# A two-layer graph network: contiguous query tiles, operands of layer 1 written in their final form by layer 0, and unit sums divided in the output stage

## The chip, the cores and the metric

The kernel runs on one core of one Trainium2 chip. A core has a matrix engine (TensorE, PE in the profile; its weight loads are PEld), VectorE (DVE), ScalarE (ACT), GpSimd (POOL), and SyncE (SP), which here only issues DMAs. The metric is device time in microseconds (us), the median over several executions. The kernel before takes 15601.34 us (three executions, 15598.64 to 15608.1).

## The reference

Two layers act on `x` (3327 nodes × 128 features) with one 0/1 matrix `adj` (3327 × 3327).

```python
# layer 0: attention by cosine over the neighbours
cos = beta[0] * (x @ x.T) / (norm2 @ norm2.T + 1e-07)
x = layernorm(x + softmax(cos + (1.0 - adj) * -1e9, axis=1) @ x)
# layer 1: d = 128, n = 3327, h = 8; q, k, v are reshaped, not transposed
q, k, v = [(x @ W.T).reshape(d, n, h) for W in (Wq, Wk, Wv)]
a = jnp.einsum('dnh,dmh->dnm', q, k) * d ** -0.5 + adj + adj
out = jnp.einsum('dnm,dmh->dnh', softmax(a, axis=2), v).reshape(n, h * d)
x = layernorm(x + out @ Wo.T)
```

Layer 1 is thus 128 dense attentions over 3327 keys, each with vectors of only 8 numbers. Its reshape mixes nodes: row-major, `x @ W.T` (3327 × 1024) is read as 128 × 3327 × 8, so one slice d takes its 3327 × 8 numbers from 26 rows of the product. The output is read back in the same way.

## The kernel before

**Names.** P = 128, N = 3327 nodes, T = 26 tiles, NP = P·T = 3328, so there is one padding node. H = 8, D = 128. Node number p·T + t stands in partition p of tile t, for queries and for keys (`node_rows`, L87, a row every T rows). `every(a, t)` (L125) picks each T-th column. Because tile 25 has only 127 real nodes, loads of it are cut in 112 + 15 partitions (`FULL`, L41) and one more.

**Layer 0** (L166 to L475, 0 to 714 us) makes 26 query tiles in a software pipeline over t: TensorE scores against all keys (`scores`), VectorE scales and masks them and finds the row's minimum, ScalarE takes logarithms and exponentials, TensorE turns the weights and multiplies by x (`turn_weights`, `weigh0`), then residual and layernorm. Each tile loads its rows of adj twice: as float32 (`raw`, SP's queue, `load` L190) and as bfloat16 (`bits`, POOL's queue, `load_bits` L201). `adj_chunk` (L209) turns the bits and stores them as `aT_s`. `project` (L348) multiplies the finished rows by Wq, Wk, Wv in six steps of 512 columns and writes rows of 1024 floats to `q_s`, `k_s`, `v_s`. POOL has almost nothing to do in this stage.

**Preparation** (`prepare`, L811 on, 714 to 989 us). For each of q and k and eight groups of 16 slices d, it loads `nat`, re-orders it on POOL (`by_t`, L819), turns it on TensorE, and splits each number in a high part rounded for TensorE and a low remainder (`high`, `low`), written to `kp_s` and `qp_s` (slice, feature, part, node). Between these steps stand the 33 first steps of the search for maxima (`first_max`).

**Main loop** (L894, 989 to 15505 us). A unit is a query block of three tiles (QB = 384 queries; the last block has two tiles) and a group of four slices d. There are 9 blocks × 32 groups = 288 units, blocks outermost. A unit makes 26 steps j, one key tile each. A step is: scores of four slices (`scores`, L704; the row-wise shift from `shifts`, adj from `add_adj`, L687), exponentials (L917 and L946 on ScalarE; for two slices adj enters as a factor on POOL, L918), and products with the values (`weigh`, L717, two steps later), which gather 9 rows a slice in `acc`: 8 features and, from a column of ones in `vt`, the sum of the weights. The search for row maxima of a later unit runs 33 steps ahead (`search`, TensorE L604, VectorE L619 to L644). It works on pairs of units, and from a known point in the first unit of a pair it needs the second one's keys.

All engines but SP follow the order in which the program is written (`manual_schedule`). SP's DMA issues stand in one queue. They are:

- `load_unit(i + 2)` at j = 2: `kx` (two DMAs), `qx` (four), `vn`; `values` at j = 14 copies `vn` into the nine-wide `vt` on POOL (L565, L566).
- at the end of a unit `take` (L726) copies `acc` to `ot` on ScalarE; at j = 8 of the next unit `values_turn` (L730) turns it by 12 small matmuls; `leave` copies the result, and `finish` (L749, j = 9) takes reciprocals, multiplies on POOL and writes `o_s` in rows of 1024.
- in the last unit of a block, `load_adj_tile` brings one tile of the next block's adj per step, and ScalarE takes its exponential five steps later (`exp_adj_tile`, L519, into `eT`).

**Output stage** (L976 to L1014). Per tile: load 128 rows of `o_s`, eight transposes (L1002), two copies (L147 on VectorE, L145 on ScalarE), eight matmuls with Wo (L1006), residual, layernorm.

Of the kernel before, what the change touches and what calls it, by code (L numbers as in the profile page):

```python
# [21 lines left out]
T = 26  # L22
# [4 lines left out]
HG = P // H  # L27
NG = D // HG
# [12 lines left out]
FULL = ((0, 112), (112, P - 1))  # L41


# [3 lines left out]
def gnn_two_layers(  # L47
# [24 lines left out]
    real = const.tile([P, 1], F32, name="real")  # L72
    nc.vector.tensor_scalar(real, ident[:, P - 1 : P], -1.0, 1.0, op0=ALU.mult, op1=ALU.add)

    q_s = dram.tile([NP, C], F32, name="q_s")
    k_s = dram.tile([NP, C], F32, name="k_s")
    v_s = dram.tile([NP, C], F32, name="v_s")
    o_s = dram.tile([NP, C], F32, name="o_s")

    qp_s = dram.tile([D, H, 2, NP], F32, name="qp_s")  # L80
    kp_s = dram.tile([D, H, 2, NP], F32, name="kp_s")
# [5 lines left out]
    def node_rows(a: bass.AP, t: int, width: int, parts: int = P, first: int = 0):  # L87

        return bass.AP(
            tensor=a.tensor,  # L90
            offset=a.offset + (first * T + t) * width,
            ap=[[T * width, parts], [1, width]],
        )

    def node_parts():

        return [(slice(a, b), T * D) for a, b in FULL] + [(slice(P - 1, P), (T - 1) * D)]

    def node_blocks(a: bass.AP, part: slice, width: int):

        return bass.AP(
            tensor=a.tensor,
            offset=a.offset + part.start * T * D,
            ap=[[T * D, part.stop - part.start], [1, width]],
        )

    def heads(a: bass.AP):

        return bass.AP(
            tensor=a.tensor,  # L110
            offset=a.offset,
            ap=[[HG * N * H, NG], [T * H, P], [N * H, HG], [1, T * H]],
        )

    def load_adj(raw, engine, t: int):

        nc.gpsimd.memset(raw[:, N:NP], PAD)
        if t < T - 1:
            engine.dma_start(raw[:, :N], node_rows(adj, t, N))
        else:  # L120
            for a, b in FULL:
                engine.dma_start(raw[a:b, :N], node_rows(adj, t, N, b - a, a))
            engine.dma_start(raw[P - 1 : P, :N], node_rows(adj, t - 1, N, 1, P - 1))
# [42 lines left out]
    with ExitStack() as l0:  # L166
# [23 lines left out]
        def load(t: int):  # L190
            u = tiles[t]
            u.raw = adj_raw.tile([P, NP], F32, name="raw")
            load_adj(u.raw, nc.sync, t)
            u.xr = ptp.tile([P, D], F32, name="xr", bufs=5)
            if t < T - 1:
                nc.sync.dma_start(u.xr, node_rows(x, t, D))
            else:
                nc.gpsimd.memset(u.xr, 0.0)
                nc.sync.dma_start(u.xr[: P - 1], node_rows(x, t, D, P - 1))

        def load_bits(t: int):  # L201

            u = tiles[t]
            u.bits = adj_raw.tile([P, NP], BF16, name="bits", bufs=2)
            load_adj(u.bits, nc.gpsimd, t)
# [49 lines left out]
        def scores(t: int, j: int):  # L255
# [4 lines left out]
            sc = score_piece(every(xT, t), xT, j)  # L260
# [87 lines left out]
        def project(t: int, k: int):  # L348
# [3 lines left out]
            if i == 0:  # L352
                u.row = ptp.tile([P, C], F32, name="row")
            cols = slice(i * 512, (i + 1) * 512)
            pq = ps_x.tile([P, 512], F32, name="pq")
            nc.tensor.matmul(pq, u.x1T, ws[n][:, cols], start=True, stop=True)
            nc.scalar.activation(
                u.row[:, cols], pq, AF.Copy, scale=float(D) ** -0.5 if n == 0 else 1.0
            )
            if i == 1:  # L360
                nc.sync.dma_start(node_rows((q_s, k_s, v_s)[n], t, C), u.row)

        with tc.manual_schedule(
# [13 lines left out]
            nc.gpsimd.memset(xs[:, T - 1, :], 0.0)  # L377
            xf = xs.rearrange("p t d -> p (t d)")
            for part, width in node_parts():
                nc.sync.dma_start(xf[part, :width], node_blocks(x, part, width))  # L380
# [10 lines left out]
            for t in range(2):  # L391
                load_bits(t)
            ws = []
            for name, wT in (("wq", wqT), ("wk", wkT), ("wv", wvT)):
                wt = big.tile([P, C], F32, name=name)
                nc.sync.dma_start(wt, wT)
                ws.append(wt)


            nc.gpsimd.tensor_mul(xs, xs, xs)  # L400
# [21 lines left out]
            nc.scalar.preload_act_table_set("natural_log_exp_and_others")  # L422

            for t in range(-2, T + 3):
# [4 lines left out]
                for k in range(8):  # L429
                    if k == 0:  # L430
# [13 lines left out]
                        if there(t - 2):  # L444
                            norm_root(t - 2)
                        continue
# [27 lines left out]
                if there(t + 4) and t + 4 > 1:  # L474
                    load_bits(t + 4)  # L475
# [8 lines left out]
    with ExitStack() as at:  # L484
# [17 lines left out]
        vts = [fix.tile([P, 4, T, H + 1], F32, name=f"vt{i}") for i in range(3)]  # L502
        for vt in vts:
            nc.gpsimd.memset(vt[:, :, :, H], 1.0)
            nc.gpsimd.tensor_copy(vt[:, :, T - 1, H], real.to_broadcast([P, 4]))
# [17 lines left out]

        def load_unit(i):
# [8 lines left out]
            kx, qx = u.kx.bitcast(F32), u.qx.bitcast(F32)  # L533
            for c in range(2):
                nc.sync.dma_start(
                    kx.rearrange("(y c) n -> c y n", c=2)[c],
                    kp_s[4 * g : 4 * g + 4].rearrange("d f r n -> (d f r) n"),
                )
                for r in range(2):
                    nc.sync.dma_start(  # L540
                        qx.rearrange("(y r c) n -> r c y n", r=2, c=2)[r, c, :, : u.nq],
# [4 lines left out]
            u.vn = keys.tile([P, 4, T, H], F32, name="vn", bufs=2)  # L546
            nc.sync.dma_start(
                u.vn.rearrange("p g t h -> p g (t h)"),
                bass.AP(
                    tensor=v_s.tensor,  # L550
                    offset=v_s.offset + 4 * g * N * H,
                    ap=[[T * H, P], [N * H, 4], [1, T * H]],
                ),
            )
            u.vt = vts[i % 3]
            if g % 2 == 0:
# [6 lines left out]
        def values(u):  # L563

            nc.gpsimd.tensor_copy(u.vt[:, :, : T - 1, :H], u.vn[:, :, : T - 1])  # L565
            nc.gpsimd.tensor_scalar(  # L566
                u.vt[:, :, T - 1, :H], u.vn[:, :, T - 1], real, None, op0=ALU.mult
# [34 lines left out]
        def max_product(u, dst, a, q, c):  # L602
# [4 lines left out]
                u.kx[rows(a), k0:k1],  # L607
# [118 lines left out]
        def take(u):  # L726
            u.ot = sm.tile([P, QB], F32, name="ot")
            nc.scalar.copy(u.ot[:, : u.nq], acc[:, : u.nq])

        def values_turn(u, dst, start):  # L730

            for q in range(u.nt):
                for c in range(4):
                    k = q * P + 32 * c
                    nc.tensor.matmul(  # L735
                        dst[32 * c : 32 * c + 32, 36 * q : 36 * q + 36],
                        u.ot[:, k : k + 32],
                        nine.rearrange("p h r -> p (h r)"),
                        start=start,
                        stop=True,  # L740
                        tile_position=(0, 32 * c),
                        skip_group_check=True,
                    )

        def leave(u, src):
            u.of = sm.tile([P, QT, 4, H + 1], F32, name="of")
            nc.scalar.copy(u.of[:, : u.nt].rearrange("p q h r -> p (q h r)"), src[:, : 36 * u.nt])

# [304 lines left out]
```

## Time and profile before

| what | us |
|---|---|
| median of three executions | 15601.34 |
| span of the profiled execution | 15611.6 |
| layer 0, last projection ends | 713.63 |
| main loop, first pb | 989.4 |
| output stage, from | about 15510 |

The profiled execution is one of its own, and its span is what the sums of a profile add up to; it is 10.3 us above the median. The page also lists the costliest groups of instructions: line, engine, operation, tile written and tiles read, shapes and count; then busy time in all and mean of one in ns; then the idle time just before them and what ended it.

```profile
L918 POOL TENSOR_TENSOR pb<-pb,eT 128x768 f32<-128x768 f32 (+1 forms) x7488 | 13190.2, 1780 | 656.3 <-ACT pb L917 374.1
L619 DVE TENSOR_REDUCE mx<-m 128x2 f32<-128x1024 f32 x6784 | 8312.5, 1225 | 970.0 <-PE eb L706 568.7
L946 ACT ACTIVATE pa<-ea 128x384 f32<-128x384 f32 (+1 forms) x14976 | 6338.4, 478 | 54.0 <-PE ea L687 14.5
```

The first line reads: 7488 multiplications on POOL, one a step, 1780 ns each, before which POOL was idle for 656 us in all, mostly until ScalarE had made `pb`.

The DMA part of the page gives each kind of transfer, with its size and its time from issue to landing:

```profile
kx<-kp_s SPq DMA_DIRECT2D x576, 832.0 KB, 6.4
vn<-v_s SPq DMA_DIRECT2D x288, 416.0 KB, 3.4
qx<-qp_s SPq DMA_DIRECT2D x1024, 48.0 KB, 4.7
```

### The profile page before, as it was taken

What the parts mean: (1) busy time and instruction counts of PE and PEld (TensorE: products, weight loads), DVE (VectorE), ACT (ScalarE), POOL (GpSimd) and SP (SyncE); (2) the same over time, 40 slices, a digit from 0 to 9 for tenths busy, and PEclk for the clock granted to TensorE, in tenths of its full rate; (3) what the DMA queues carried; (4) which work ended last, traced back from release to release, by engine and by line L of the source; (5) the groups of instructions that cost most, each with busy time, mean ns of one, the idle gap of its engine ahead of it and who ended that gap; (6) DMA issues with size and microseconds to landing.
All of it is one profiled execution on the core that took longest, in us unless ns stands there. A gap on an engine that the chain in (4) does not pass through costs nothing.

```text
span 15611.6 us, 508271 instructions
## 1 busy us (share of the span) xinstructions
PE 15342.4 (98%) x217532; PEld 6892.6 (44%) x217532; DVE 13898.5 (89%) x16311; ACT 12601.3 (81%) x24955; POOL 13899.2 (89%) x9625
## 2 busy tenths in 40 slices
PE   8879999999999999999999999999999999999999
PEld 6634444444444444444444444444444444444555
DVE  7679999999999999999999999999999999998776
ACT  7658888888888888888888888888888888888776
POOL 0059999999999999999999999999999999999886
PEclk9879999999999999999999999999999999999999
DMA  7651111111111111111111111111111111111112
GB/s 207 204 199 47 48 51 53 50 46 50 52 51 46 50 49 54 50 46 50 53 50 46 50 53 49 50 46 56 46 50 46 50 53 50 48 48 60 60 58 75
DMA packets 631082, 973.65 MB, mean 62 GB/s; under 512 B 283568, under 2 KB 545838, under 8 KB 588368
## 3 DMA queue, kind: packets, MB, share of 16 engines
q1 hardware_dynamic: 625024, 918.99, 18.3%
q0 software_dynamic: 3792, 22.15, 0.8%
q8 instruction: 1703, 27.90, 0.8%
q14 instruction: 563, 4.61, 0.1%
HBM read 828.48 MB, written 134.61 MB: 62 GB/s over the span
## 4 chain that ended last, share of the span: by engine, by line
PE 93%; DVE 0%; issue 0%; ACT 0%; DMA 0%; POOL 0%; SPq 0%; POOLq 0%; ACTq 0%; DVEq 0%
PE acc L717 30%; PE ea L687 21%; PE m L604 16%; PE eb L700 13%; PE ea L700 10%; PE ea L706 2%; PE ea L673 1%; PE ea L735 1%; PE eb L706 1%; PE pp L1006 0%; DVE oT L147 0%; DMA qp_s<-low 0%; ACT pa L946 0%; PE tp L157 0%; DVE hid L1008 0%
## 5 line engine op out<-in xcount | busy, mean ns | idle before, releaser
L918 POOL TENSOR_TENSOR pb<-pb,eT 128x768 f32<-128x768 f32 (+1 forms) x7488 | 13190.2, 1780 | 656.3 <-ACT pb L917 374.1
L619 DVE TENSOR_REDUCE mx<-m 128x2 f32<-128x1024 f32 x6784 | 8312.5, 1225 | 970.0 <-PE eb L706 568.7
L917 ACT ACTIVATE pb<-eb 128x768 f32<-128x768 f32 (+1 forms) x7488 | 5894.9, 787 | 2497.9 <-PE eb L706 1784.2
L604 PE MATMUL m<-kx,qx 32*128 32x512 f32 (+1 forms) x23296 | 6873.5, 472 | 80.5 <-DVE mx L619 71.5
L946 ACT ACTIVATE pa<-ea 128x384 f32<-128x384 f32 (+1 forms) x14976 | 6338.4, 478 | 54.0 <-PE ea L687 14.5
L717 PE MATMUL acc<-pb,vt 128*9 128x384 f32 (+1 forms) x29952 | 5901.1, 474 | 0.1
L717 PE MATMUL acc<-pa,vt 128*9 128x384 f32 (+1 forms) x29952 | 5901.1, 474 | 0.0
L640 DVE TENSOR_REDUCE mx<-m 128x1 f32<-128x512 f32 x6400 | 4360.3, 681 | 258.5 <-PE m L604 239.9
L700 PEld LDWEIGHTS <-one 3*128 3x128 bf16 x29952 | 1469.1, 91 | 5634.9 <-issue 4656.0
L687 PE MATMUL ea<-aT,two 128*32 128x384 bf16 (+1 forms) x59904 | 3714.8, 325 | 0.0
L706 PE MATMUL eb<-qx,kx 32*128 32x384 f32 (+1 forms) x14976 | 3422.3, 453 | 0.0
L706 PE MATMUL ea<-qx,kx 32*128 32x384 f32 (+1 forms) x14976 | 3326.9, 434 | 0.0
L604 PEld LDWEIGHTS m<-kx,qx 32*128 32x128 f32 x23296 | 2825.0, 182 | 315.0 <-DVE mx L619 80.0
L700 PE MATMUL ea<-cx,one 3*128 3x384 bf16 (+1 forms) x14976 | 2744.1, 324 | 1.0
L700 PE MATMUL eb<-cx,one 3*128 3x384 bf16 (+1 forms) x14976 | 2464.3, 326 | 4.6 <-ACT pb L917 3.8
L717 PEld LDWEIGHTS acc<-pa,vt 128*9 128x9 f32 x29952 | 1412.0, 91 | 398.9
L717 PEld LDWEIGHTS acc<-pb,vt 128*9 128x9 f32 x29952 | 1411.5, 91 | 386.8 <-POOL pb L918 0.6
L687 PEld LDWEIGHTS <-two 128*32 128x32 bf16 x59904 | 945.2, 95 | 1364.4 <-issue 1171.4
L706 PEld LDWEIGHTS eb<-qx,kx 32*128 32x128 f32 x14976 | 1432.7, 188 | 0.0
L706 PEld LDWEIGHTS ea<-qx,kx 32*128 32x128 f32 x14976 | 1396.3, 182 | 7.3 <-issue 3.7
L644 DVE TENSOR_REDUCE mx<-m 128x2 f32<-128x512 f32 x1088 | 742.9, 683 | 20.6 <-PE m L604 19.3
L630 DVE TENSOR_REDUCE mx<-m 128x4 f32<-128x1024 f32 x288 | 352.8, 1225 | 46.7 <-PE m L604 28.6
(130 smaller groups left out, 4899.0 us busy)
## 6 DMA issues: line engine op xcount, KB each, us to landing
kx<-kp_s SPq DMA_DIRECT2D x576, 832.0 KB, 6.4
vn<-v_s SPq DMA_DIRECT2D x288, 416.0 KB, 3.4
qx<-qp_s SPq DMA_DIRECT2D x1024, 48.0 KB, 4.7
raw<-in_adj_dram SPq DMA_DIRECT2D x25, 1663.5 KB, 6.5
aT_s<-aT SPq DMA_DIRECT2D x26, 832.0 KB, 9.8
bits<-in_adj_dram POOLq DMA_DIRECT2D x25, 831.8 KB, 7.2
aT<-aT_s SPq DMA_DIRECT2D x208, 96.0 KB, 2.1
q_s<-row SPq DMA_DIRECT2D x26, 512.0 KB, 7.6
```

What stands on the lines that cost most here:

```text
L604: nc.tensor.matmul(dst, u.qx[rows(a), q * P : (q + 1) * P], u.kx[rows(a), k0:k1], start=True, stop=True,)
L619: nc.vector.tensor_reduce(u.mx[:, h, qs[0], c], m, axis=AX.X, op=ALU.max)
L630: nc.vector.tensor_reduce(dst, m.rearrange("p a (x k) -> p a x k", x=2), axis=AX.X, op=ALU.max)
L640: nc.vector.tensor_reduce(u.mx[:, a, qs[0], c : c + 1], m, axis=AX.X, op=ALU.max)
L644: nc.vector.tensor_reduce(u.mx[:, a, qs[0] : qs[1] + 1, c], m.rearrange("p (q k) -> p q k", q=2), axis=AX.X, op=ALU.max,)
L687: nc.tensor.matmul(e[r, : u.nq], two[:, r], aT[:, j, : u.nq], start=False, stop=True, tile_position=(0, 32 * c), skip_group_check=True,)
L700: nc.tensor.matmul(e[:, : u.nq], one[r], u.cx[r, : u.nq], start=True, stop=False, skip_group_check=True)
L706: nc.tensor.matmul(e[:, : u.nq], u.kx[rows(a), j * P : (j + 1) * P], u.qx[rows(a), : u.nq], start=False, stop=stop, skip_group_check=True,)
L717: nc.tensor.matmul(acc[32 * h : 32 * h + H + 1, : u.nq], u.vt[:, h, j], pts[h][:, : u.nq], start=(j == 0), stop=(j == T - 1), tile_positio ...
L917: nc.scalar.activation(pt_b[:, :, : u.nq], e_b[:, :, : u.nq], AF.Exp)
L918: nc.gpsimd.tensor_tensor(pt_b[:, :, : u.nq], pt_b[:, :, : u.nq], eT[:, j, : u.nq].unsqueeze(1).to_broadcast([P, 2, u.nq]), ALU.mult,)
L946: nc.scalar.activation(pt_a[:, h, : u.nq], e[:, : u.nq], AF.Exp)
```

## The change

Query tiles become plain: tile t holds nodes 128·t to 128·t + 127, the last 127 (`LAST`) and a copy of the last one. Keys stay in steps of T in the main loop (partition p of tile t is node p·T + t).

Layer 0's `project` splits q and k itself (POOL copies and subtracts) and writes `qn_s`, `kn_s` (part, feature, flat position); Wq and Wk are re-ordered once so that a feature's columns lie together. v is written nine wide with its ones. The bits of adj are cast from `raw` on POOL instead of loaded. The preparation goes. Instead, `gather` copies each group's q and k between tensors in DRAM; a unit of the first block loads its keys in natural order (`kn`, tile `km`), searches on those, and ScalarE orders them into `kx` (`order_keys`, one tile a step, in the unit before), which `keep_keys` writes to `kp_s` for the later blocks. `vt` is loaded by two DMAs of 127 partitions and 1. The unit's nine rows a slice go to `o_s` undivided, by four DMAs, and the output stage takes the reciprocals and multiplies.

```diff
+LAST = N - (T - 1) * P
...
-            for a, b in FULL:
-                engine.dma_start(raw[a:b, :N], node_rows(adj, t, N, b - a, a))
-            engine.dma_start(raw[P - 1 : P, :N], node_rows(adj, t - 1, N, 1, P - 1))
+            engine.dma_start(raw[:LAST, :N], rows_of(adj, t, N, LAST))
+            engine.dma_start(raw[LAST:P, :N], rows_of(adj, t, N, P - LAST, LAST - 1))
...
-            u.bits = adj_raw.tile([P, NP], BF16, name="bits", bufs=2)
-            load_adj(u.bits, nc.gpsimd, t)
+            u.bits = adj_raw.tile([P, NP], BF16, name="bits", bufs=1)
+            nc.gpsimd.tensor_copy(u.bits, u.raw)
...
+            high = ptp.tile([P, 512], F32R, name="high")
+            low = ptp.tile([P, 512], F32R, name="low")
+            nc.gpsimd.tensor_copy(high, row)
+            nc.gpsimd.tensor_tensor(low, row, high.bitcast(F32), ALU.subtract)
+            dst = (qn_s, kn_s)[n]
+            for c, part in enumerate((high, low)):
+                nc.sync.dma_start(
+                    bass.AP(
+                        tensor=dst.tensor,
+                        offset=dst.offset + (c * H + 4 * i) * S2 + t * P * P,
+                        ap=[[P, P], [S2, 4], [1, P]],
+                    ),
+                    part.bitcast(F32).rearrange("p (f s) -> p f s", f=4),
+                )
...
-            nc.gpsimd.tensor_mul(xs, xs, xs)
+            nc.gpsimd.tensor_mul(xs, xn, xn)
...
+        def gather(g):
+
+            def heads_of(a, c, first, n):
+
+                return bass.AP(
+                    tensor=a.tensor,
+                    offset=a.offset + c * H * S2 + 4 * g * N + first,
+                    ap=[[N, 4], [S2, H], [1, n]],
+                )
+
+            for c in range(2):
+                nc.sync.dma_start(qp_s[4 * g : 4 * g + 4, :, c], heads_of(qn_s, c, 0, NP))
+                dst = kq_s[4 * g : 4 * g + 4, :, c]
+                nc.sync.dma_start(dst[:, :, :N], heads_of(kn_s, c, 0, N))
+                nc.sync.dma_start(dst[:, :, N:NP], heads_of(kn_s, c, N - 1, NP - N))
...
             u.vt = vts[i % 3]
+            for first, n, rows in ((0, P - 1, T), (P - 1, 1, N - (P - 1) * T)):
+                nc.sync.dma_start(
+                    u.vt.rearrange("p g t r -> p g (t r)")[first : first + n, :, : rows * R9],
+                    bass.AP(
+                        tensor=v_s.tensor,
+                        offset=v_s.offset + (4 * g * N + first * T) * R9,
+                        ap=[[T * R9, n], [N * R9, 4], [1, rows * R9]],
+                    ),
+                )
...
+        def order_keys(u, j):
+
+            nc.scalar.copy(u.kx[:, j * P : (j + 1) * P], every(u.km.bitcast(F32), j))
+
+        def keep_keys(u):
+
+            nc.sync.dma_start(
+                kp_s[4 * u.g : 4 * u.g + 4].rearrange("d f r n -> (d f r) n"),
+                u.kx.bitcast(F32).rearrange("(y c) n -> c y n", c=2)[0],
+            )
...
-            u.ot = sm.tile([P, QB], F32, name="ot")
-            nc.scalar.copy(u.ot[:, : u.nq], acc[:, : u.nq])
...
+            ot = sm.tile([P, QB], F32, name="ot")
+            nc.scalar.copy(ot[:, : u.nq], acc[:, : u.nq])
+            n = min(u.nq, N - u.b * QB)
+            for h in range(4):
+                nc.sync.dma_start(
+                    bass.AP(
+                        tensor=o_s.tensor,
+                        offset=o_s.offset + (4 * u.g + h) * N + u.b * QB,
+                        ap=[[S2, R9], [1, n]],
+                    ),
+                    ot[32 * h : 32 * h + R9, :n],
+                )
...
+                    if j == 12 and i + 4 < G4:
+                        gather(i + 4)
...
-                    if j == 8 and done is not None:
-                        values_turn(done, free, False)
-                        copies.append(lambda: leave(done, free))
-                    if j == 9 and done is not None:
-                        copies.append(lambda: finish(done))
...
+                    if x is not None and not x.b:
+                        order_keys(x, j)
+                        if j == T - 1:
+                            keep_keys(x)
...
+            rec = work.tile([P, P], F32, name="rec")
+            nc.vector.reciprocal(rec, row[:, H, :])
+            nc.gpsimd.tensor_tensor(
+                row[:, :H, :], row[:, :H, :], rec.unsqueeze(1).to_broadcast([P, H, P]), ALU.mult
+            )
```

Before the loop, the changed kernel gathers groups 0 to 3, loads units 0 and 1, orders the keys of unit 0 on POOL in one copy, and makes the 33 first search steps with the exponentials of block 0's adj between them. In the output stage a tile of `o_s` is loaded as 128 partitions × 9 × 128, in packets of 512 B.

## The prediction

> **What bounds the kernel now.** I read the busy shares, the chain of waits, then the busy time by stretch, one stretch per stage.
>
> ```profile
> PE 15342.4 (98%) x217532; PEld 6892.6 (44%) x217532; DVE 13898.5 (89%) x16311; ACT 12601.3 (81%) x24955; POOL 13899.2 (89%) x9625
> ...
> PE 93%; DVE 0%; issue 0%; ACT 0%; DMA 0%; POOL 0%; SPq 0%; POOLq 0%; ACTq 0%; DVEq 0%
> ```
>
> And the windows: length, busy PE, PEld, DVE, ACT, POOL (with instructions), granted clock, DMA share, GB/s.
>
> ```profile
> 500.00:600.00 100.00, 95.18 (x572) 74.83 (x573) 90.10 (x133) 86.44 (x113) 4.07 (x15) 1.00 0.78 220
> 800.00:850.00 50.00, 21.41 (x86) 15.66 (x86) 27.24 (x42) 13.71 (x27) 8.87 (x3) 0.57 1.00 337
> 1500.00:2500.00 1000.00, 999.88 (x14391) 422.78 (x14388) 921.57 (x1044) 822.88 (x1608) 958.46 (x637) 1.00 0.15 49
> 15500.00:15612.00 112.00, 86.86 (x768) 75.92 (x765) 50.37 (x183) 28.23 (x70) 6.95 (x7) 0.95 0.53 158
> ```
>
> The main loop, 989 to 15505 us, is bound by TensorE (999.88 of 1000), with POOL at 96%. Layer 0, to 714, is nearly bound by TensorE and VectorE together, POOL idle. The preparation, 714 to 989, is bound by DMA (share 1.00) and leaves TensorE 43% busy. So work removed from TensorE in the loop is worth its full time, the preparation is worth its length, and a wait in the loop costs what it exceeds its slack by.
>
> **What goes: −236.** (a) Preparation. The stage takes 275 us. What must stay is the first 33 search steps: 33 × 2.11 (three successive ones end at 813.92, 816.02, 818.14) = 70. Ahead of them the first keys (`kn`): SP issues them once the v_s write eight transfers earlier is done, and that write's packets stand, on one engine, behind the `vt` of units 0 and 1 (22 us each, below), of which about 36 are still to run. Then 7 for the load, and 3 to start the loop: 116. Gain 159.
> (b) The turn of the unit sums. In the chain:
>
> ```profile
> 8037.19 0.65 PE acc L717 x8
> ...
> 8038.66 0.39 PE ea L735 x24
> 8039.05 0.33 PE ea L687 x8
> 8039.38 0.65 PE acc L717 x8
> ```
>
> Step 8 takes 2.19 us from acc to acc (8037.19 to 8039.38), the neighbours 1.94 to 1.97. 0.235 × (256 full units + 32 × 2/3) = 65. The copy, products and writes that L747 to the end of `finish` made goes too, beside TensorE.
> (c) Startup. POOL's square (L400) waits for a second load of x until 29.35; the first is there by 15. −12.
>
> **One DMA engine for 127 rows.** Five transfers of the changed kernel have 127 partitions: `raw` and `xr` of tile 25, every unit's `vt`, the last `orow`, the last of `out`. The trace has the `xr`:
>
> ```profile
> 598.11 0.43 SPq L122 DMA_DIRECT2D raw<-in_adj_dram  x1
> 598.59 0.66 SPq L123 DMA_DIRECT2D raw<-in_adj_dram  x1
> 599.35 0.23 SPq L199 DMA_DIRECT2D xr<-in_x_dram  x1
> ```
>
> The 112-row `raw` at L122 raises its semaphore 16 times, once for each DMA engine; the `xr` of 127 rows raises it once at issue and once more, at 607.16: one engine carried it. [...] Packets here: 13,308 B take 498 ns, 832 B 39, 512 B 27; so 936 B about 43 (estimate).
>
> **What comes.** (d) `raw` of tile 25: 127 × 0.498 = 63 us where 112 + 15 rows took about 9. It is issued three tiles ahead, some 11 to 15 us beyond its present need: +52 (35 to 70).
> (e) Layer 0 on POOL: four copies of 512 columns (L565: 0.86 for 800, so 0.55), four subtractions (1.04, L418) and a cast of 3328 columns (2.96, L819) per tile, 9.3 us where POOL did under 1. In the trace POOL is free, so by idle time alone they cost nothing. [...]
>
> ```profile
> L244 DVE SCALAR_TENSOR_TENSOR n<-norm_k,norm_c,y 128x1664 f32<-128x1664 f32 x34 | 66.1, 1945 | 0.0
> L251 DVE SCALAR_TENSOR_TENSOR y<-n,y 128x1664 f32<-128x1664 f32 x34 | 64.2, 1887 | 0.6
> ...
> L264 DVE CUSTOM_DVE_ANT_0 s<-s,raw,mn 128x832 f32<-128x832 f32 x51 | 55.3, 1085 | 3.7
> ```
>
> Per tile 2 × 1.95 + 2 × 1.89 + 4 × 1.07 = 12.0 of 23.56 us. [...] If 9.3 us of POOL fall at random on that 51%, 4.7 us are lost; VectorE's idle 2.4 absorbs half. That is +2.3 a tile, × 24 = +55, where idle time alone says 0 (range 0 to 115, no absorption).
> (f) First block. The keys come in natural order and ScalarE re-orders them, 26 copies of 128 columns a unit for 31 units. In SP's order a unit's loads (`kn`, `qx`) now stand behind `keep_keys` and the four sums writes, both waiting on ScalarE. Before, the order was
>
> ```profile
> 6107.98 0.46 SPq L535 DMA_DIRECT2D kx<-kp_s  x1
> 6108.49 1.23 SPq L540 DMA_DIRECT2D qx<-qp_s  x2
> 6109.76 0.59 SPq L535 DMA_DIRECT2D kx<-kp_s  x1
> 6110.40 1.23 SPq L540 DMA_DIRECT2D qx<-qp_s  x2
> ```
>
> for a unit that begins (its first pb) at 6109.57; the last lands at 6116.95, and the search that needs both units of a pair starts 9.0 in: slack 1.7. Issued after the sum copy (ends 3.9 in), four writes at 0.37, and six gathers' remains, the last lands about 14.7 in: 5.7 late, in the 15 pairs: +85, the last unit +4. The copies themselves: block transitions already carry 26 more ACT exponentials of 540 ns:
>
> ```profile
> 4196.80:4248.40 51.60, 51.60 (x747) 21.59 (x742) 47.57 (x55) 42.59 (x83) 49.49 (x34) 1.00 0.15 49
> 4248.47:4300.31 51.84, 51.84 (x751) 22.02 (x746) 47.66 (x55) 49.85 (x104) 49.55 (x34) 1.00 0.33 95
> ```
>
> 0.24 × 31 = +7, doubled for the strided read. Together +104 (50 to 250).
> (g) Later blocks, odd units: `qx` halves behind the sums writes land 8.4 to 9.5 in against 9.0: +10 (0 to 80).
> (h) Block transitions. `vt`'s 127 partitions of 4 rows are 508 packets × 43 ns = 22 us on one engine, issued about 8 in, until about 32. The tiles of adj queued behind it (the third on) use the same engine among others; ScalarE's exponential of the third is due 15.4 in and stands in order before the step's own exponentials. 16.5 × 7 transitions + 13 for the first = +128 (60 to 200). Elsewhere the 22 us lie beside 51.7 us of compute and cost nothing; if that cover is gone, (f)'s upper end.
> (i) Output stage. Now 3.36 us a tile, TensorE:
>
> ```profile
> L1006 PE MATMUL pp<-wo,oT 128*128 128x128 f32 x416 | 54.9, 286 | 10.9 <-DVE oT L147 10.9
> ...
> L147 DVE COPY oT<-otp 128x512 f32<-128x512 f32 x26 | 17.5, 675 | 8.1 <-PE otp L1002 8.1
> ```
>
> Added: a reciprocal of 128 columns (L753 takes 219 ns for 12, L407 316 for 26: about 0.95) and POOL's product of 1024 (L918 takes 1.78 for 768: about 2.3). The next tile's reciprocal stands on VectorE behind this tile's oT copy, so tiles chain: 0.95 + 2.3 + 0.64 for four transposes + 0.68 copy + 0.6 of hand-overs = 5.15. 1.8 × 25 = +45 (19 to 50). The last tile's 127 × 9 packets at 27 ns are 31 us on one engine, about 10 of it prefetched: +21; final write +2: +68 (30 to 100).
> At nothing: fewer DMAs on POOL's queue, narrower v (ACT at 86% in layer 0 keeps its count), eight more SP issues per tile (SP idle most of the tile), the vt copies and divisions leaving POOL.
>
> **Sum.** −159 − 65 − 12 = −236; +52 + 55 + 104 + 10 + 128 + 68 = +417. Net +181. From the profiled 15611.6 that is a span of 15,793; the runs' median stands 10.3 below that span, so **15,782 us**.
>
> **Rivals.**
> *A, the other side: 127 rows are spread over many engines* (chance 0.1). Then (d), (h) and the last tile's 21 fall away, and the backlog of 36 before the first keys too: −272 + 55 + 104 + 10 + 47 = −56: 15,545. It decides once a 127-partition transfer completes from several engines. For: the `xr` is 65 KB in small packets, and no large transfer of 127 rows is in the trace. Against: its single record.
> *B, ScalarE becomes the bound of the first block* (0.15): 26 strided copies a unit, each some 0.15 us beyond ScalarE's idle time of a step: 806 × 0.15 = +121: 15,903. For: 42.59 of 51.60 busy before they come; against: 26 exponentials more cost 0.24.
> *C, nothing absorbs the port lock of layer 0* (0.1): 4.7 a tile: 15,840. [...]
> *D, the gathers saturate an engine* (0.15). [...]
> The forecast itself has 0.5.
>
> **How the numbers follow.** A measurement here tells 0.2% (31 us) from no change. Of A's 0.1 half ends faster than that; the other half, and the forecast's lowest tail, within it. Faster 0.06, same 0.05, slower 0.89. Range 15,640 to 16,010: low ends of (f), (h) and (i) together take 140 off; above, B, C and part of D are in. Some 0.2 is left out: A and the worse half of D.
>
> **What would show it.** Loop start near 920 with two TensorE gaps, one at tile 25 of layer 0. Windows with L735 gone and a middle unit of 51.45. Seven transitions of about 68 us, ACT waiting there for aT. Odd units of block 0 near 57, PE waiting on `qx`. An output stage with tiles 5.1 us apart. Wrong if 127-row `vt` lands in under 10 us, if layer 0's VectorE operations keep their means while POOL works, or if block 0's units all exceed 55.

## The result, and the profile after

The changed kernel takes 15823.11 us (15820.36 to 15836.9, four runs) beside 15604.72 us for the one before on the same chip: a ratio of 1.0142, 95% interval 1.0127 to 1.0156. Its profiled execution has a span of 15820.7 us, 209 above the 15611.6 of before (the medians are 218 apart). The forecast was a median of 15,782 and a span of 15,793.

The page of the changed kernel, busy time by engine and then the chain of work that ended last:

```profile
PE 15277.7 (97%) x210460; PEld 6710.8 (42%) x210460; DVE 13944.4 (88%) x15903; ACT 12741.1 (81%) x25361; POOL 13786.9 (87%) x8952
...
PE 92%; DVE 2%; DMA 2%; SPq 1%; issue 1%; ACT 1%; POOL 0%; POOLq 0%; DVEq 0%; ACTq 0%
```

TensorE has 65 us less to do (15342.4 before), and the chain, which was TensorE and nothing else, has got shares of DVE, DMA and SPq, SP's queue. Busy windows of the changed kernel, with the columns of the prediction:

```profile
500.00:600.00 100.00, 87.09 (x487) 60.88 (x485) 90.42 (x114) 74.34 (x100) 38.08 (x34) 0.95 0.67 199
680.00:760.00 80.00, 30.33 (x156) 20.82 (x155) 27.50 (x40) 25.74 (x33) 15.26 (x13) 0.68 0.28 80
...
4329.86:4398.82 68.96, 53.46 (x727) 22.46 (x722) 47.54 (x54) 49.83 (x104) 48.13 (x31) 0.88 0.26 74
15660.00:15820.00 160.00, 80.72 (x628) 73.48 (x624) 105.99 (x208) 22.07 (x54) 61.07 (x26) 0.88 0.43 120
```

Layer 0 keeps VectorE at 90%, but gets through fewer instructions with it (114 in 100 us, 133 before). Around tile 25 all engines stand for most of 80 us. The transition of 68.96 us contains nearly the same work as the one of 51.84 before. The output stage is now longer, and TensorE is busy in half of it.

From the starts of the `pb` exponentials and of the score pieces of layer 0, the time splits up as follows.

| stretch (us) | before | after | difference |
|---|---|---|---|
| start to the first score piece of layer 0 | 72.9 | 57.0 | −15.9 |
| from there to layer 0's last projection | 640.7 | 789.9 | +149.2 |
| from there to the first pb | 275.8 | 107.5 | −168.3 |
| block 0 of the main loop | 1656.3 | 1779.2 | +122.9 |
| blocks 1 to 7 | 11579.0 | 11652.2 | +73 |
| block 8, to the last pb | 1280.8 | 1271.9 | −9 |
| last pb to the end | 106.1 | 163.1 | +57 |

The clock that TensorE was granted is lower in the stages where it waits: 0.68 around tile 25, 0.88 in the transition and in the output stage (the third number from the end of each row above), 0.95 in layer 0. What the lower clock adds to a loss isn't separated from the wait itself.

### The profile page after: what moved, and what is told of

Read it like the earlier page. It is cut to its first block, busy times and chain, and to the rows that moved or that the text cites. A ratio compares the mean times of both kernels' runs of the same rounds, so it can differ in the third digit from the quotient of the medians.

```text
span 15820.7 us, 494570 instructions
## 1 busy us (share of the span) xinstructions
PE 15277.7 (97%) x210460; PEld 6710.8 (42%) x210460; DVE 13944.4 (88%) x15903; ACT 12741.1 (81%) x25361; POOL 13786.9 (87%) x8952
## 4 chain that ended last, share of the span: by engine, by line
PE 92%; DVE 2%; DMA 2%; SPq 1%; issue 1%; ACT 1%; POOL 0%; POOLq 0%; DVEq 0%; ACTq 0%
PE acc L747 29%; PE ea L717 21%; PE m L634 16%; PE eb L730 12%; PE ea L730 9%; PE ea L736 1%; PE ea L703 1%; SPq L574 1%; DMA qx<-qp_s 1%; DVE s L236 0%; PE acc L277 0%; PE eb L736 0%; PE pq L329 0%; DMA aT<-aT_s 0%; DVE w L306 0%
## 5 line engine op out<-in xcount | busy, mean ns | idle before, releaser
L881 ACT ACTIVATE pa<-ea 128x384 f32<-128x384 f32 (+1 forms) x14976 | 6338.7, 478 | 29.7 <-PE ea L717 16.6
L634 PE MATMUL m<-kx,qx 32*128 32x512 f32 (+1 forms) x20608 | 6081.7, 472 | 4.6 <-DMA qx<-qp_s 4.1
L634 PEld LDWEIGHTS m<-kx,qx 32*128 32x128 f32 x20608 | 2495.5, 181 | 198.7 <-issue 5.1
L634 PE MATMUL m<-kn,qx 32*128 32x512 f32 (+1 forms) x2688 | 805.6, 490 | 131.7 <-DMA qx<-qp_s 107.7
```

Of the source, the lines that this page charges most:

```text
L634: nc.tensor.matmul(dst, u.qx[rows(a), q * P : (q + 1) * P], u.km[rows(a), k0:k1], start=True, stop=True,)
L881: nc.scalar.activation(pt_a[:, h, : u.nq], e[:, : u.nq], AF.Exp)
```

## The experiments

Each kernel is the changed one with the edit that is shown, and was timed beside the kernel before (15,595 to 15,610 us by the batch of runs). Differences below are against that kernel in the same batch; the change itself stands at +218.

**The 127 rows of the values.** The first experiment cuts one transfer:

```diff
-            for first, n, rows in ((0, P - 1, T), (P - 1, 1, N - (P - 1) * T)):
+            for first, n, rows in ((0, 112, T), (112, 15, T), (P - 1, 1, N - (P - 1) * T)):
```

> Every unit's values are loaded as 112 + 15 + 1 partitions instead of 127 + 1; nothing else changes. Theory (127 rows go to one DMA engine): the transfer no longer holds up the queue for 17 to 20 us, so the last unit of each block falls from 66 to 71 us to about 51.7; eight of them give -140, a time near 15,683. The odd units of block 0 stay near 59, since their loads are late for another reason (their place in SP's queue). Rival 1 (the exponentials on ScalarE, or the adj loads themselves, make the transition slow): nothing moves, 15,823. Rival 2 (the loaded engine is also what delays the odd units of block 0): these fall as well, by up to 7 us each, and the time goes to about 15,580.

Measured: 15664.09 us, +54 (ratio 1.0035, 1.0022 to 1.0048). The transitions of blocks 1 to 7 fall from 66 to 70 us to 49.4 to 52.3, that of block 0 from 71.4 to 57.6. The odd units of block 0 stay at 59.3 (58.8 before the cut): rivals 1 and 2 fall. The first pb comes 28.5 us earlier too (925.9 for 954.4), the backlog that the prediction put at 36 and this expectation left out.

How the wait arises is seen in SP's own timeline, the transition of the changed kernel at 4329.86 (start, duration of the issue, line, transfer, count):

```profile
4335.25 0.34 SPq L520 DMA_DIRECT2D aT<-aT_s  x1
4335.64 1.09 SPq L564 DMA_DIRECT2D qx<-qp_s  x2
4337.07 17.59 SPq L574 DMA_DIRECT2D vt<-v_s  x2
4355.09 2.71 SPq L520 DMA_DIRECT2D aT<-aT_s  x6
```

The issues around it take 0.3 to 0.6 us each. Of the 17.59 us at L574, the 127 rows take 0.23 and the single row after them 17.31, although that is one row. It doesn't wait for its semaphore, which the eighth DMA before it, an `o_s` write, had left by 4336.91; when its issue ends, 392 of the 508 packets of the 127 rows have started. The third tile of adj, `aT`, stands behind it on SP's queue. In the run with the cut the three issues at this place take 1.53 us, and `aT` follows at once.

The blocked issue is what the eye finds first, but it is not what ends the wait. The chain of waits goes on through the transfer, and ScalarE's exponential of the third tile starts when it has landed:

```profile
4355.09 6.09 DMA aT<-aT_s
```

```profile
4361.20 0.52 ACT L524 ACTIVATE eT<-aT 128x384 f32<-128x384 bf16 x1 [16.00 <-DMA aT<-aT_s]
```

The semaphore of this `aT` counts 16 landings, one for each share of the transfer. Of these, 15 have come by 4357.27, 2.2 us after its issue. The last comes at 4361.18, 0.41 us after the 127 rows have (4360.77; their semaphore rises once at issue and once here). In all eight transitions it comes 0.41 to 0.43 us after them. So this share stood behind the 127 rows on their DMA engine, as the prediction had it. The blocked issue runs beside that wait, and what it would cost alone no run separates.

At tile 25 of layer 0, in the changed kernel, the issues are blocked too:

```profile
672.64 0.27 SPq L97 DMA_DIRECT2D raw<-in_adj_dram  x1
672.96 29.66 SPq L98 DMA_DIRECT2D raw<-in_adj_dram  x1
702.72 1.90 SPq L174 DMA_DIRECT2D xr<-in_x_dram  x1
704.71 35.24 SPq L194 DMA_DIRECT2D aT_s<-aT  x1
```

The 127 rows at L97 are issued in 0.27 us, the one row at L98 takes 29.66, and, once `xr` has added another 127 packets, the write of `aT_s` takes 35.24. It ends at 739.95, 67.3 us after L97 (127 × 0.498 = 63 us). Here as well the first wait is for the data: POOL's cast needs `raw`, whose 127 rows land at 739.55 and whose single row lands at 740.10.

```profile
740.25 2.96 POOL L180 CAST bits<-raw 128x3328 bf16<-128x3328 f32 x1 [55.63 <-DMA raw<-in_adj_dram]
```

The late write of `aT_s` then holds ScalarE's next copy into `aT` until 746.17, about 2.5 us after the first bits were turned.

**Is it the number 127?** The same loop with `((0, 126, T), (126, 1, T), (P - 1, 1, ...))`:

> The values are loaded as 126 + 1 + 1 partitions, everything else as in the changed kernel. [...] Rival (a transfer of over 112 or of any number not divisible by 16 goes to one or few engines): transitions stay over 60 us, 15,750 or more.

Measured: 15647.58 us, +53 (1.0035, 1.0020 to 1.0049); transitions 49.4 to 51.9, that of block 0 58.4. One row fewer in the transfer is as good as the cut in 112 and 15 (+54), so the rival falls: no limit at 112 or need of a multiple of 16 is there. Beyond these three cuts no run tells which numbers of rows do well.

**The other transfers of 127 rows**, cut in the way of the kernel before:

```diff
-            engine.dma_start(raw[:LAST, :N], rows_of(adj, t, N, LAST))
+            for a, b in FULL:
+                engine.dma_start(raw[a:b, :N], rows_of(adj, t, N, b - a, a))
```

and `xr`, the last `orow` and the last rows of `out` alike.

> The adj rows and x rows of tile 25, the last rows of the unit sums and the last rows of the output are moved as 112 + 15 partitions. Theory: the one long tile of layer 0 (74.4 us where its neighbours take 27.4) falls to about 28, -47; the last tile of the output stage comes about 15 to 20 us earlier; together -62 to -67, about 15,758. Rival (the gap of tile 25 comes from the gathers between DRAM tensors that begin there, or from VectorE's waits for POOL): at most -20, 15,803.

Measured: 15760.55 us, +151 (1.0097, 1.0081 to 1.0112), 63 to 67 less than the change. The tile of 74.4 us takes 28.7. In the output stage the gap before the last tile but one falls from 27.4 to 5.1 us, and 20 us are saved there.

**VectorE beside POOL's work.** Two operations of VectorE in layer 0 (200 to 600 us), in the kernel before and then in the changed one:

```profile
L264 DVE CUSTOM_DVE_ANT_0 s<-s,raw 128x832 f32<-128x832 f32 x17 | 17.4, 1025 | 2.6 <-DVE s L261 0.5
L331 DVE TENSOR_TENSOR w<-r 128x1 f32<-128x1 f32 x17 | 2.6, 150 | 0.0
```

```profile
L306 DVE TENSOR_TENSOR w<-r 128x1 f32<-128x1 f32 x14 | 32.2, 2301 | 0.0
L239 DVE CUSTOM_DVE_ANT_0 s<-s,raw 128x832 f32<-128x832 f32 x15 | 30.6, 2042 | 2.0
```

The timelines of POOL and of VectorE at the same time, in the changed kernel:

```profile
403.88 3.77 POOL L180 CAST bits<-raw 128x3328 bf16<-128x3328 f32 x1
407.60 0.61 POOL L351 CAST high<-row 128x512 fp32r<-128x512 f32 x1
408.29 1.28 POOL L352 TENSOR_TENSOR low<-row,high 128x512 fp32r<-128x512 f32 x1
```

```profile
405.36 2.30 DVE L306 TENSOR_TENSOR w<-r 128x1 f32<-128x1 f32 x1
407.70 0.52 DVE L307 TENSOR_TENSOR w<-w,var 128x1 f32<-128x1 f32 x1
408.25 0.15 DVE L308 TENSOR_SCALAR w<-w 128x1 f32<-128x1 f32 x1
408.44 1.14 DVE L309 TENSOR_TENSOR r<-r,w 128x1 f32<-128x1 f32 x1
```

L306 squares one number in each partition. It took 150 ns before; here it takes 2.30 us and ends at 407.66, just as POOL's cast ends (407.65). In all 14 tiles of this window it ends 13 to 17 ns after the cast. L307 ends with the first `high`, L309 with `low`. L308 takes 0.15 us, as it did before (154 ns by the mean in both kernels). The profile counts the longer durations as busy time (2301 ns for L306, with 0.0 idle ahead of it), which is why VectorE looks as full as ever. By their means in 200 to 600 us, five operations lose per tile 2.15 (L306), 0.36 (L307), 0.98 (L309), 0.24 (x1, L311) and 1.02 (the first `s<-s,raw`, L239, 2042 ns for 1025): 4.75 us. Tiles take 27.4 to 28.9 us where they took 23.6. All five stand near the start of a tile, on the way to the next scores.

The cast is then taken away, on top of `e2_rows`:

```diff
-        def take_bits(t: int):
+        def load_bits(t: int):
 
             u = tiles[t]
             u.bits = adj_raw.tile([P, NP], BF16, name="bits", bufs=1)
-            nc.gpsimd.tensor_copy(u.bits, u.raw)
+            load_adj(u.bits, nc.gpsimd, t)
...
+                if there(t + 3) and t + 3 > 0:
+                    load_bits(t + 3)
```

> As e2_rows, and the bits of adj are loaded by their own DMA on POOL's queue again (one buffer) instead of cast from the float rows on POOL. Theory (VectorE and POOL exclude each other): the first of the small VectorE operations, 2.30 us behind the cast where it took 0.15, is back under 0.6; the one on the first score piece stays near 2.0 and the later ones keep about 1 us of stall, since the split of q and k remains. A tile falls from about 28.0 to 25.5 to 26, 22 tiles give -45 to -55 against e2_rows, about 15,707. Rival (layer 0 is slower because of its DMA traffic, eight writes in packets of 512 B a tile): the extra load makes it no faster, 15,758 or more. Rival 2 (the single bits buffer comes late): TensorE waits for bits, and the tile stays at 27 or more although VectorE's stalls go.

Measured: 15718.73 us, +109 (1.0069, 1.0054 to 1.0084), 42 less than `e2_rows` (45 to 55 expected); the first pb comes at 861.6 for 906.5. The groups of VectorE and POOL in 200 to 600 us of this run (busy us, mean ns):

```profile
L242 DVE CUSTOM_DVE_ANT_0 s<-s,raw 128x832 f32<-128x832 f32 x15 | 24.3, 1620 | 2.0
...
L309 DVE TENSOR_TENSOR w<-r 128x1 f32<-128x1 f32 x16 | 4.8, 297 | 0.0
...
L312 DVE TENSOR_TENSOR r<-r,w 128x1 f32<-128x1 f32 x16 | 2.6, 159 | 0.6
```

```profile
L355 POOL TENSOR_TENSOR low<-row,high 128x512 fp32r<-128x512 f32 x61 | 109.4, 1794 | 5.3 <-DMA qn_s<-low 0.3
```

The small operations are nearly back at their old times (297 and 159 ns), and the first score piece loses 0.6 instead of 1.0. Now POOL's `low` is the longer one: it takes 1794 ns where it took 1273. Tiles take 24 to 32 us, 25.8 on the average for 27.8, so the traffic rival falls as the cause of the whole, but 2.2 us a tile are still lost. Part is VectorE again: `n`, an operation of 1664 columns, takes 2240 ns for 1945. Another part is a wait for a DMA, from the waits of this run in 200 to 700 us:

```profile
ACT aT L194 <- DMA aT_s<-aT: 21.8, 7, 6.4
```

In the four longest tiles (28 to 32 us) ScalarE waits some 4.6 us before it can fill `aT` again, until the last write from it has landed, and TensorE stands behind it. The kernel before has no such wait there. The DMA engines are busier with the bits on them (a share of 0.89 in 200 to 600 us, 0.69 in `e2_rows`). TensorE's and ScalarE's waits show none for the single bits buffer.

**The order on SP's queue in block 0.** The changed kernel at an odd unit, which starts at 1228.10 (its first pb), SP's timeline:

```profile
1228.05 0.51 SPq L595 DMA_DIRECT2D kp_s<-kx  x1
1232.48 1.62 SPq L761 DMA_DIRECT2D o_s<-ot  x4
1234.22 0.51 SPq L559 DMA_DIRECT2D kn<-kq_s  x1
1234.83 1.17 SPq L564 DMA_DIRECT2D qx<-qp_s  x2
1236.05 0.58 SPq L559 DMA_DIRECT2D kn<-kq_s  x1
1236.68 1.23 SPq L564 DMA_DIRECT2D qx<-qp_s  x2
1238.01 20.86 SPq L574 DMA_DIRECT2D vt<-v_s  x2
```

The keys are issued 6.1 us in, behind the sums writes that wait for ScalarE. In the chain of waits of this unit the last `qx` is in flight from 1237.32 for 6.03 us, to 1243.35, 15.25 us in; it is needed 9.0 in. The odd units 3 to 29 take 58.85 us on the average, the even ones 51.54.

Three attempts were made to get the loads out from behind the writes. The first gives the writes to another queue (`nc.scalar.dma_start` in `take` and `keep_keys`):

> The writes of the unit sums and of the ordered keys are issued on ScalarE's queue instead of SP's; nothing else changes. Theory (the loads of the next pair stand in SP's queue behind writes that wait for ScalarE): the 14 odd units of block 0 that take 58 to 60 us fall to 51.6 to 52, -100 to -105; the five issues cost ScalarE some 1.7 us a unit, beside TensorE, 0 to +20; time near 15,725. Transitions stay near 69. Rival (the gathers and the values saturate one DMA engine): the loads land as late as before, the odd units stay over 57, 15,815 or more.

Measured: 16807.23 us, +1198 (1.0772, 1.0754 to 1.0790). Both views were wrong on the price. The units of blocks 1 to 7 take 2.6 us more on the average (54.06 for 51.48). ScalarE stands there for four issues in each, of 0.33 us by the median, just ahead of an exponential that TensorE and POOL wait for, and this exponential waits 1.7 us for them (13.9 us, eight times, in 3000 to 3400 us). In block 0 there is a fifth. Six units of the last block take 64 to 67 us; the cause of that is open. In block 0 the loads were still late, for a reason that belongs to neither view: the DMAs of both queues share eight semaphores in turn, and so one of SP's gathers waited for the keys' write on ScalarE's queue, whose semaphore it shares, with the loads behind it. In the unit from 1243.77 the write is issued at 1243.20 and lands at 1248.85, and the gather is issued at 1248.86. In the trace of the changed kernel, where SP issues all 4316 DMAs, none is issued before the eighth one ahead of it has landed (16 ns after it at the least). This run says nothing on the gathers.

The second calls `load_unit` a step earlier:

```diff
-                    if j == 2 and i + 2 < NU:
+                    if j == 1 and i + 2 < NU:
                         us[i + 2] = load_unit(i + 2)
```

> load_unit is called one step earlier (j = 1 instead of 2), which puts the loads of a unit of block 0 ahead of the sums writes in SP's queue, but still behind the writing of the ordered keys; all DMAs stay on SP's queue. Theory (place in the queue): kn is issued about 0.5 after a unit's start instead of 6.1, the last qx lands about 9 to 10 in where 15.2 was measured and 9.0 is needed, and the 14 odd units fall from 58 to 60 us to 51.6 to 53: -80 to -105, near 15,730. Rival (gathers and values saturate one DMA engine, so that loads land late wherever they are issued): the odd units stay over 57, 15,815. Transitions stay near 69.

Measured: 23711.5 us (1.5218, 1.5184 to 1.5251). The edit was not what it was meant to be. At j = 1 the last product of unit i − 1 is still to come, and it reads the buffer that `load_unit(i + 2)` fills. With the load ahead of it in the program, the product waits for the load and uses the values of a later unit: the kernel no longer computes the same thing. The waits of this run in 6000 to 6400 us (engine, line, releaser: sum, times, longest) show it:

```profile
ACT ot L758 <- PE acc L747: 128.0, 5, 26.7
PE acc L747 <- DMA vt<-v_s: 124.5, 5, 26.0
```

TensorE stands about 25 us in every unit, the 127 rows on their way. The same edit is in the first kernel that joins the cures, where the values are cut in 112 and 15 and the wait is shorter, though paid in every unit:

> All cures together: values, adj rows, output rows in 112 + 15 parts (e1_vt, e2_rows), bits of adj by DMA (e3_bits), loads one step earlier (e5_early), output stage in the order of e6_out. If the losses are separate and add up: 15,719 (e3_bits) - 159 (e1_vt) - 90 - 27 = about 15,443, 1.0% faster than the kernel before the change. If they overlap (a wait hidden behind another one), 15,500 or more.

Measured: 18405.17 us (1.1793, 1.1776 to 1.1810), full-width units of 59 to 65 us. It tells nothing on the sum of the cures.

The third leaves the loads where they were, and calls the writes later:

```diff
+                    if j == 4 and done is not None:
+                        send(done)
+                        if not u.b:
+                            keep_keys(u)
...
                         order_keys(x, j)
-                        if j == T - 1:
-                            keep_keys(x)
```

where `send` is the four `o_s` writes of `take`, which keeps only the copy.

> In place of e5_early, whose edit put the load of the values ahead of the last product that reads their buffer: load_unit stays at j = 2, and the writes of the unit sums and of the ordered keys are called at j = 4, so that a unit's loads stand ahead of both on SP's queue. Theory (place in the queue): kn is issued at about the start of a unit instead of 6.1 in, the last qx lands 7.5 to 9 in, and the 14 odd units of block 0 fall from 58 to 60 us to 51.6 to 52.5: -90 to -105, near 15,725. Rival (gathers and values saturate one DMA engine): the odd units stay over 57. Transitions stay near 69.

Measured: 15708.84 us, +103 (1.0068, 1.0053 to 1.0083), 115 less than the change; block 0 falls from 1779.2 to 1669.7 us. SP's timeline of the same unit, which now starts at 1210.68:

```profile
1210.63 0.51 SPq L559 DMA_DIRECT2D kn<-kq_s  x1
1211.24 1.17 SPq L564 DMA_DIRECT2D qx<-qp_s  x2
1212.46 0.58 SPq L559 DMA_DIRECT2D kn<-kq_s  x1
1213.10 2.11 SPq L564 DMA_DIRECT2D qx<-qp_s  x2
1215.31 19.91 SPq L574 DMA_DIRECT2D vt<-v_s  x2
```

The keys and the `qx` are all issued within 4.6 us, the last `qx` lands 9.0 in, and the odd units take 51.4 to 51.9 us. The gathers, the values on one engine and ScalarE's ordering of the keys are all still there, so rivals B and D of the prediction are out as well. The transitions stay at 65 to 68.

**The output stage.** The prediction had a tile's reciprocal, product, transposes and copy in one chain. The order was written out by hand to break it:

```diff
+            for t in range(T + 2):
+                if t < T:
+                    divide(t)
+                if 0 <= t - 1 < T:
+                    turn_rows(t - 1)
+                if 0 <= t - 2:
+                    combine(t - 2)
```

with the load, reciprocal and product in `divide`, the transposes and copies in `turn_rows`, and the rest in `combine`.

> Only the order of the output stage is changed, written out by hand: a tile's reciprocal and product run one tile ahead of its transposes, two ahead of its matmuls. Theory (a tile's reciprocal, product, transposes and copy form one serial chain of 4.61 us): tiles come every 3.4 to 3.6 us, TensorE bound as before the change, -24 to -30; the last tile keeps its 23 us for the 127 rows; near 15,796. Rival (VectorE's or POOL's own time, or the loads in packets of 512 B, set the 4.61): no gain, 15,823.

Measured: 15806.42 us, +211 (1.0134, 1.0120 to 1.0147). Tiles come in turns of 3.44 and 4.71 us, a mean of 4.08 for 4.61; in all the stage is 7 us shorter, where 24 to 30 were expected. The timeline of all engines in the changed kernel shows what the 4.61 was made of (rows between left out):

```profile
15698.82 2.35 POOL L940 TENSOR_TENSOR orow<-orow,rec 128x1024 f32<-128x1024 f32 x1 [2.26 <-DVE ln_rstd L111]
15699.18 2.08 DVE L114 TENSOR_SCALAR res<-hid,ln_mv,ln_rstd 128x128 f32<-128x128 f32 x1
...
15701.18 0.28 DVE L953 TENSOR_TENSOR hid<-pp,x1r 128x128 f32<-128x128 f32 x1
...
15702.38 0.92 DVE L939 RECIPROCAL rec<-orow 128x128 f32<-128x128 f32 x1
...
15703.43 2.35 POOL L940 TENSOR_TENSOR orow<-orow,rec 128x1024 f32<-128x1024 f32 x1 [2.26 <-DVE ln_rstd L111]
```

The last step of the layernorm (L114) takes 2.08 us and ends with POOL's product. That is so in 23 of the 26 tiles, each time within 0.1 us; in the other three no product runs, and it takes 0.35. This looks like L306 beside the cast again. L114 reads one tile and two numbers per partition; which of these makes it wait was not separated. The ring is product 2.35, then on VectorE `hid`, statistics and copy, 1.2, reciprocal 0.92, and POOL's next product: 4.61, without a transpose in it. In the order written by hand L114 is short (0.34 us), and another ring shows in that trace: product 2.35 (at 15719.91), transposes (15722.31), matmuls (15723.24), `hid` and layernorm (15725.23), reciprocal (15726.99), product (15728.07), 8.16 us for two tiles.

**All cures.** The parts of `e1_vt`, `e2_rows`, `e3_bits`, `e8_defer` and `e6_out`, with six buffers for the tiles of the output stage:

> The cures of e1_vt, e2_rows, e3_bits, e8_defer and the output order of e6_out with six instead of three buffers for its tiles. If the losses are separate and add up: 15,719 (e3_bits) - 159 (e1_vt) - 95 (e8_defer) - 20 = about 15,445, 1.0% faster than the kernel before the change. If they overlap (a wait hidden behind another one), 15,500 or more.

Measured: 15428.99 us, −176 (0.9888, 0.9871 to 0.9904), 16 below the expected sum and 1 from what the five runs measured one by one (+109 with `e2_rows` and `e3_bits`, then 164, 115 and 7 less: −177). The losses add up. The output tiles still take 4.08 us, so the buffers were not what held them. With the product one tile further ahead (`turn_rows(t - 2)`, `combine(t - 3)`):

> e9_all with the reciprocal and product of the output stage two tiles ahead of the transposes instead of one. Theory (in e6_out and e9_all the ring product, transposes, matmuls, layernorm, next reciprocal takes 8.15 us and carries two tiles, hence 4.08 a tile): with three tiles on the ring, TensorE's 3.4 us set the pace, -15 to -17, about 15,413. Rival (the loads, or POOL's or VectorE's own time): no gain.

Measured: 15396.21 us, −199 (0.9872, 0.9857 to 0.9887). Tiles come every 3.43 us. This is the fastest version, 1.3% faster than the kernel before the change. Its window in layer 0:

```profile
500.00:600.00 100.00, 90.93 (x517) 63.89 (x517) 87.04 (x128) 78.69 (x100) 46.73 (x43) 0.97 0.88 242
```

POOL is busy 47 of 100 us there, and VectorE at 128 instructions is still below the 133 of before. From its first score piece to its last projection layer 0 takes 685.5 us, 45 more than before. About half of that are four tiles of 29 to 31 us, in which ScalarE waits for the write of `aT_s` as in `e3_bits` (21.6 us in 200 to 700 us). The splitting of q and k on POOL, left in, probably accounts for most of the rest; no run takes it out.

## Why the prediction was right

The measured 15,823 us are 41 above the forecast of 15,782. Their nearness is in part luck: (e) came out 47 us dearer than forecast, and (a), (c), (d), (g) and (i) together some 39 better. The result is nearer to rival C's 15,840, which had a chance of 0.1, and C's premise is what came true.

**(a) to (c), the gains, 236 forecast.** The preparation gave 168 (159 forecast). The backlog before the first keys is 28.5 us by the cut in 112 and 15, and 37 by the one in 126 and 1 (36). The start gave 15.9 (12). TensorE's step without the 24 small products shows in plain units of 51.45 us for 51.67, 0.22 less (0.235). The first and the last came out a little larger than forecast, the step a little smaller.

**(d) raw of tile 25: +52 forecast, 47 measured** (74.4 for 27.4). The one engine and the wait for `raw` were as forecast. That SP stands at the following issues was not foreseen; it adds about 2.5 us.

**(e) layer 0, VectorE beside POOL: +55 forecast, +102 measured** (149.2 less the 47 of (d)). That POOL's work holds VectorE's up is shown by the ends of L306 (13 to 17 ns after the cast's) and by the run without the cast, which gave back 42 us; that it makes up the rest of the 102 is argued from the stalls, since no run takes the splitting out. No run shows the term as it was forecast, POOL's 9.3 us falling at random on large operations and half of the loss absorbed; the runs showed 4.75 us a tile lost in five operations. The forecast's 4.7 came so near by luck: of the operations it counted, `n` and `y`, 7.7 of its 12 us, lost nothing (1945 and 1888 ns). Three operations on single numbers, which it didn't count, lost 3.5. Half of the stall was to be absorbed by VectorE's idle 2.4. Hardly any was: VectorE is idle 2.4 us a tile after the change and 2.5 before, and tiles are 4.4 us longer. The stalls fall at a tile's start, while the idle time lies ahead of score pieces that TensorE brings. This was rival C, and it is the term that puts the span 28 us above the forecast.

**(f) block 0: +104 forecast.** The odd units 3 to 29 lose 14 × 7.3 = 102, and unit 1 loses 6 more; `e8_defer` takes 109.5 off the block. The landing was forecast 14.7 in and was 15.25. Ordering the keys costs about 0.1 us a unit (51.54 for 51.45), less than the 0.24 to 0.5 allowed; no run shows the doubling for the strided read, an assumption of the forecast.

**(g) later odd units: +10 forecast, 0 measured** (51.4 to 51.5, as their neighbours).

**(h) transitions: +128 forecast.** Cut in 112 and 15, they lose 136 us: 17.4 for each of seven, 13.9 for the first. The mechanism was as forecast, down to its times: the 508 packets follow one another at 44 ns each (43 estimated), the 127 rows land 30.9 us in (about 32), and the exponential due at about 15.4 waits 16.0 for the share of `aT` that stands behind them on their engine (16.5). That SP's queue is blocked meanwhile was not foreseen.

**(i) output stage: +68 forecast, +57 measured.** Tiles take 4.61 us (5.15), the last one waits 23 us more (21). The chain forecast for the tiles was wrong in its parts, as shown above: POOL's product and the VectorE operation that ends with it, and not the transposes, close it.

Rival A fell with the first view of the transitions; B and D fell with `e8_defer`.

Two lines were read loosely in the prediction, without an effect on its sums. The L122 at 598.11 is the 15-row part of `raw`, whose semaphore rises once at issue and 15 times later; the 112 rows were issued at 593.81, and theirs rises 16 times. The three search times are starts of steps, not ends.

## What to carry to other kernels

A transfer of 127 partitions landed 66.9 us after its issue began (`raw`) and 23.7 us (`vt`), and the last of 16 landings of a later transfer came 0.41 to 0.43 us after that: look for 127 rows where tiles are cut, and cut them as 112 + 15 or 126 + 1, with which the transitions fell from 66 to 70 us to 49.4 to 52.3. Idle time on POOL was no free room beside VectorE in layer 0 (+102 us); the loss stood in longer durations of small VectorE operations (0.15 to 2.30 us), with no wait reported, and here it was not made up by idle time elsewhere in the tile. A DMA that waits for a late engine should be issued after the loads of the next unit, on the same queue (15,708.84 us for 15,823.11; on ScalarE's queue 16,807.23).

## What the runs showed of the hardware that was not expected

- After a transfer of 127 rows, an issue behind it on the queue blocked: 17.3 us behind 508 packets of 936 B, 29.7 and 35.2 us behind 127 packets of 13,308 B. A transfer of a single row was held up too (17.31 and 29.66 us). The next large transfer had 15 of its 16 landings 2.2 us after its issue, and the sixteenth only 0.4 us after the 127 rows had landed.
- POOL's work held up a VectorE operation on one number per partition (L306, from 0.15 to 2.30 us), and a scaling with numbers from SBUF (L114, from 0.35 to 2.08 us), not only large ones.
- Four DMA issues a unit on ScalarE's queue, of 0.33 us by the median, made units 2.6 us longer on the average (54.06 for 51.48), though ScalarE is 81% busy.
